# A conv–attention block in fp32 on one core: the order of the second pass, the last band's taps, and the place of its contraction

## The chip, the cores and the metric

The kernel runs on one core of one Trainium2 chip. The metric is the device time of one execution in microseconds, the median of several runs. Before the change: 3298.57 us, the median of three (3298.3 to 3300.13).

## The reference

The input is 8 images of 384 channels and 64 x 64 pixels, all in float32. Two layers follow each other, each added to its input:

```python
x = x + L0(_gn(x), Wq, bq, Wk, bk, Wv, bv, Wfc, bfc)     # linear attention
x = x + L1(_gn(x), fft_filter, w_in, w_dw, w_out)        # filter, depthwise conv, gate

# L0: conv1x1 = a 384 x 384 matrix over the channels, plus a bias; 6 heads of 64
q, k, v = rope(conv1x1(x, Wq, bq)), rope(conv1x1(x, Wk, bk)), conv1x1(x, Wv, bv)
q, k = elu(heads(q) * scale) + 1, elu(heads(k)) + 1
kv, k_sum = einsum('bhnd,bhne->bhde', k, v), k.sum(axis=2)
out = einsum('bhnd,bhde->bhne', q, kv) / (einsum('bhnd,bhd->bhn', q, k_sum) + 1e-6)
y0 = conv1x1(out, Wfc, bfc)
# L1
t = einsum('bchw,oc->bohw', x, w_in)
t = irfft2(rfft2(8 x 8 blocks of t) * fft_filter)
t = depthwise 3 x 3 convolution of t with w_dw, zero padding
y1 = einsum('bchw,oc->bohw', gelu(t[:, :192]) * t[:, 192:], w_out)
```

`_gn` is a group normalisation over 32 groups of 12 channels and all pixels. The keys and values of an image must be summed over all pixels before any output of L0 can be formed, and L0's result must be known over all pixels before L1's normalisation.

## The kernel before

An image is cut into 8 bands of 8 rows (512 pixels); a tile holds 384 channels as 3 blocks of 128 partitions by 512. Work on an image has a first pass (keys, values, their products; `k_project`, `v_project`, `kv_accumulate`), a second pass (`queries`, one call per image) and the L1 stage (the loop over `j` under `for b in range(nb)`). The first pass of image b+1 is woven into L1 of image b, so that TensorE has matmuls at all times. The last image's L1 has its own loop at the end.

The second pass handles a band in four steps. `q_project` (tile `pq`, 18 matmul records a band; every fp32 matmul shows as two) projects the queries, VectorE turns them (`turn`, L667, and L682, L684) and ScalarE and VectorE apply elu (`elu_plus_one`). `q_normalise` (tile `pn`) multiplies them with the key sums; VectorE and ScalarE form the reciprocal and split it into bfloat16 pieces (`rn`, `part`, `parts`, L701 to L709). `q_spread` (tile `prb`) spreads `parts` over the channels with bfloat16 matmuls and multiplies q by it on VectorE (L726). `project_out` (tile `pf`, 18 records a band) forms the product with the folded matrix `mt`; VectorE adds it to x (L738, `latest["sum"]`), and `band_sums` takes the statistics for L1's normalisation on ScalarE (L180, L183), the values of band 0 on VectorE.

Other work runs along in that pass. `late` is a generator, `last_band(b)`, with what remains of the previous image's last band of L1: its depthwise taps, gate and contraction; `next(late, None)` does one step of it. A tap is one of nine shifted products of the 3 x 3 filter: on VectorE one instruction per block of 128 channels (`tile_taps`, L839), or on ScalarE into a tile that a POOL transfer adds to the sum (`add_tap`, L823 and L825). `late_w` is a copy of the tap weights by way of a matmul with the identity (`pwd`). `chain` is `layer0_chain(b + 1)`: the next image's normalisation in small steps on VectorE (`far_chain`) with POOL transfers through DRAM in between, then the scaling of the key weights and the bias rows (`kvbias`).

After the second pass, `norm_chain(b, 1)` forms L1's normalisation in four steps (tiles `ps_m`, `ps_mc`, `ps_v`, `ps_r`, each with VectorE work behind it); between them `more` puts matmuls of the next image's keys (`pk`). Then `normalised` (tile `hf`) and the first matmuls of L1 (`pi`) follow. `contraction` (tile `pw`) is L1's last product; where the x tile is gone, its result is copied to `y` and a POOL transfer adds it to the output in DRAM.

The order on each engine is a planner's: it goes by the order of the text as priority and moves an instruction forward where by its own estimate the engine is free and the inputs are there. Within a block under `tc.issue_after(ins)`, instructions on the engine of `ins` come behind `ins`. `next(...)` on a generator does its work up to the next `yield`, so the `yield`s set the places in the text. PSUM has 8 tiles (`ps_tile`), the pool of work tiles `w` 9, that of `x` tiles 10, that of depthwise tiles `dw` 2.

## Time and profile before

The profiled execution took 3298.98 us; its span from the first to the last instruction is 3297.2 us.

| | busy us | share of the span |
|---|---|---|
| TensorE matmul (PE) | 3249.1 | 99% |
| TensorE weight load (PEld) | 1823.3 | 55% |
| VectorE (DVE) | 2724.7 | 83% |
| ScalarE (ACT) | 2040.4 | 62% |
| GpSimd (POOL) | 253.8 | 8% |

The granted clock of TensorE is 0.996 of full speed over the span. Matmuls are pipelined and their ends are modelled, so a record is longer than the distance to the next start; distances between starts are used below for what a group costs. A wait "A <- B" is the time that engine A stood idle until B's result came. "Issue" or a missing releaser means that the engine waited for nothing that the profile shows. SP issues the loads and stores, POOL the transfers that add and the small ones of the normalisation.

### The profile page before, as it was taken

Reading aid. Unit: us, or ns where it says so; the run is one execution under the profiler, and the core shown is the slowest. Engines: PE = TensorE matmul, PEld = TensorE weight load, DVE = VectorE, ACT = ScalarE, POOL = GpSimd, SP = SyncE. Lnnn points to the kernel's source line nnn. Section 1 sums busy time; section 2 is a strip of 40 time slices with the busy share of each in tenths; the row PEclk is TensorE's granted clock in tenths of the full one; section 3 lists DMA queues with packets and bytes.
Section 4 is the critical chain, followed back from the end, with each engine's and each line's share of the span. In section 5 each row is a group of like instructions: output and inputs, shape, how many; then the busy total and the mean of one; then the engine's idle time right before and its main releaser. Section 6 shows DMA issues by size and latency. Waiting matters only on the chain.

```text
span 3297.2 us, 53257 instructions
## 1 busy us (share of the span) xinstructions
PE 3249.1 (99%) x21133; PEld 1823.3 (55%) x21133; DVE 2724.7 (83%) x4480; ACT 2040.4 (62%) x4065; POOL 253.8 (8%) x381
## 2 busy tenths in 40 slices
PE   8999999999999999999999999999999999999998
PEld 5544666455664566645665456654566545665455
DVE  6577789978889789896888968899689987888767
ACT  4445666656766566655767556666566665556675
POOL 0000000000000000100001000010000100000064
PEclk9999999999999999999999999999999999999999
DMA  6324234452344524435235343354334542334113
GB/s 219 114 86 119 88 86 111 135 138 74 97 117 119 145 58 116 114 115 142 72 93 139 109 123 87 90 135 119 113 78 104 135 115 75 78 68 119 71 30 58
DMA packets 154445, 346.33 MB, mean 105 GB/s; under 512 B 29812, under 2 KB 41060, under 8 KB 146004
## 3 DMA queue, kind: packets, MB, share of 16 engines
q1 hardware_dynamic: 124500, 282.65, 26.3%
q0 software_dynamic: 29504, 60.06, 12.3%
q8 instruction: 166, 2.72, 0.3%
q14 instruction: 83, 0.68, 0.1%
q10 hardware_dynamic: 192, 0.21, 0.0%
HBM read 235.62 MB, written 99.93 MB: 102 GB/s over the span
## 4 chain that ended last, share of the span: by engine, by line
PE 92%; DVE 3%; ACT 3%; issue 1%; DMA 0%; SPq 0%; POOL 0%; DVEq 0%; ACTq 0%; POOLq 0%
PE pf L734 15%; PE pi L752 15%; PE pk L491 15%; PE pv L507 13%; PE pq L655 13%; PE pw L933 5%; PE pb L789 3%; PE pw L944 3%; PE acc L523 3%; PE pd L768 3%; PE acc L536 2%; PE pn L693 1%; ACT mt L570 1%; PE prb L717 1%; PE sums L865 1%
## 5 line engine op out<-in xcount | busy, mean ns | idle before, releaser
L839 DVE SCALAR_TENSOR_TENSOR dw<-ring,w_dw,dw 128x512 f32<-128x512 f32 x1225 | 858.7, 747 | 231.8 <-ACT ring L805 196.4
L491 PE MATMUL pk<-wk,x 128*128 128x384 f32 x1536 | 544.7, 496 | 0.0
L655 PE MATMUL pq<-x,wq 128*128 128x512 f32 x1152 | 521.6, 601 | 2.6 <-ACT mt L570 2.6
L752 PE MATMUL pi<-w_in,hf 128*128 128x384 f32 x1536 | 513.5, 491 | 5.5 <-ACT ring L799 4.2
L734 PE MATMUL pf<-qc,mt 128*128 128x512 f32 x1152 | 510.7, 597 | 0.0
L507 PE MATMUL pv<-wv,x 128*128 128x384 f32 x1344 | 470.0, 488 | 0.0
L752 PEld LDWEIGHTS pi<-w_in,hf 128*128 128x128 f32 x1536 | 288.0, 190 | 199.1 <-ACT ring L799 5.0
L491 PEld LDWEIGHTS pk<-wk,x 128*128 128x128 f32 x1536 | 283.5, 191 | 205.2 <-issue 32.2
L514 ACT COPY v<-pv 128x384 f32<-128x384 f32 x224 | 108.7, 485 | 424.5 <-PE pv L507 423.2
L734 PEld LDWEIGHTS pf<-qc,mt 128*128 128x128 f32 x1152 | 214.3, 190 | 255.5 <-issue 239.6
L507 PEld LDWEIGHTS pv<-wv,x 128*128 128x128 f32 x1344 | 253.6, 190 | 181.4 <-issue 8.4
L655 PEld LDWEIGHTS pq<-x,wq 128*128 128x128 f32 x1152 | 212.8, 190 | 250.6 <-issue 226.2
L738 DVE SCALAR_TENSOR_TENSOR x<-pf,bfc,x 128x512 f32<-128x512 f32 x192 | 138.6, 743 | 83.6 <-PE pf L734 83.2
L379 ACT ACTIVATE qs<-qc 128x512 f32<-128x512 f32 (+1 forms) x128 | 107.0, 836 | 144.1 <-DVE qc L684 143.7
L963 POOL DMA_DIRECT2D out_dram<-y x63 | 80.9, 1284 | 1446.6 <-DVE dw L839 799.0
L180 ACT ACTIVATE differences<-x,shift 128x512 f32<-128x512 f32 x168 | 120.0, 714 | 105.5 <-DVE x L738 105.5
L933 PE MATMUL pw<-gated,w_out 128*128 128x256 f32 x768 | 177.7, 380 | 3.2 <-DVE gated L849 2.0
L494 DVE TENSOR_TENSOR kc<-pk,kvbias 128x384 f32<-128x384 f32 x256 | 140.7, 550 | 40.6 <-PE pk L491 40.6
L933 PEld LDWEIGHTS pw<-gated,w_out 128*128 128x128 f32 x768 | 144.9, 190 | 43.7 <-issue 10.3
L759 ACT COPY ht<-pi 128x384 f32<-128x384 f32 x256 | 114.7, 483 | 68.2 <-PE pi L752 64.4
L379 ACT ACTIVATE ks<-kc 128x1536 f32<-128x1536 f32 x64 | 95.0, 1485 | 95.5 <-DVE kc L498 95.0
L374 ACT ACTIVATE hf<-x,nb,rs 128x512 f32<-128x512 f32 x192 | 146.1, 808 | 2.3 <-DVE nb L319 2.3
(216 smaller groups left out, 4555.4 us busy)
## 6 DMA issues: line engine op xcount, KB each, us to landing
tq<-in_tq SPq DMA_DIRECT2D x64, 1024.0 KB, 4.7
x<-in_x SPq DMA_DIRECT2D x64, 768.0 KB, 5.9
tk<-in_tk SPq DMA_DIRECT2D x64, 768.0 KB, 4.3
out_dram<-x SPq DMA_DIRECT2D x63, 768.0 KB, 3.5
out_dram<-y POOLq DMA_DIRECT2D x63, 768.0 KB, 7.7
xs<-in_x SPq DMA_DIRECT2D x56, 768.0 KB, 5.9
dw<-tap POOLq DMA_DIRECT2D x14, 512.0 KB, 6.4
wk<-in_wk SPq DMA_DIRECT2D x8, 576.0 KB, 3.8
```

The costliest lines, as they stand in the source:

```text
L180: nc.scalar.activation(out[:, m, :], x_[:, m, :], AF.Identity, bias=shift[:, m : m + 1], accum_out=of_m[0])
L374: nc.scalar.activation(dst, src, AF.Identity, bias=nb_[:, t : t + 1], scale=rs[:, t : t + 1])
L379: nc.scalar.activation(e, x_, AF.Relu, scale=-1.0)
L491: nc.tensor.matmul(pk[:, :C], tokens(t), wks[:, t, :], start=(t == 0), stop=(t == CT - 1))
L494: nc.vector.tensor_add(kc[:, i, :], pk[:, :C], bias)
L507: nc.tensor.matmul(pv[:, :C], xt[b, j][:, t, i * P : (i + 1) * P], wvs[:, t, :], start=(t == 0), stop=(t == CT - 1),)
L655: nc.tensor.matmul(p_, wqs[:, t, m * P : (m + 1) * P], xt[b, j][:, t, :], start=(t == 0), stop=(t == CT - 1),)
L734: nc.tensor.matmul(p_, mt[:, t, m * P : (m + 1) * P], q[:, t, :], start=(t == 0), stop=(t == CT - 1))
L738: latest["sum"] = nc.vector.scalar_tensor_tensor(xm, p_, bfc[:, m : m + 1], xm, ALU.add, ALU.add).ins
L752: nc.tensor.matmul(p_[:, :C], h[:, t, i * P : (i + 1) * P], w_in[:, t, :], start=(t == 0), stop=(t == CT - 1),)
L839: nc.vector.scalar_tensor_tensor(acc[:, m], src, wd, acc[:, m], ALU.mult, ALU.add)
L933: nc.tensor.matmul(p_[h][:, m - m0, :], w_out[:, 0, m * P : (m + 1) * P], gated[:, h * HT : (h + 1) * HT], start=(m == m0), stop=False,)
```

## The change

In `queries`, bands 2 to 7: the queries of band j+2 are projected without a cut, then band j-1's output product, then band j's spread, and band j+1's `q_normalise` directly behind it (for the last image from band 5 on, spread before output). The first spread comes behind the first third of band 3's queries. At band 7, two quarters of the next image's band 0 keys are projected ahead of the output product and the last spread; their VectorE work is put behind `parts`.

In `last_band`: taps 1 to 4 of all three blocks on ScalarE with a POOL transfer each, where it was taps 1 and 2 of two blocks; `late_w` and `pwd` go; VectorE's taps come behind the band's sum (block 0) or behind `parts` (blocks 1 and 2), the gate behind the last tap. The contraction of the last band moves to the norm chain of the following image, and its result is copied into the depthwise tile (`spare`) instead of an x tile.

In `far_chain` one `yield` moves, and the transfer of the shift is issued ahead of the read-back of the other; the scaling of the key weights and the bias columns come behind the last band's turned queries (`queried`); the scaling of the query weights behind the filter of band 4 in L1 (`filtered`). The first two loads of the next image's x are one band earlier.

```diff
@@ -333,7 +333,6 @@
         yield
-        yield
         mean, var = at[:, :, 0], at[:, :, 1]
@@ -355,10 +354,14 @@
         nc.gpsimd.dma_start(line.rearrange("(g k) -> g k", g=NG), var)
+        shift = scratch.tile([NG], F32, tag="shift", name=f"shift_line_{b}")
+        nc.gpsimd.dma_start(shift.rearrange("(g i) -> g i", i=1), minus)
         rs = small.tile([P, CT], F32, tag="rs0", name=f"rs0_{b}")
         nc.gpsimd.dma_start(rs, line.rearrange("(t p) -> p t", p=P))
-        params += rs, shift_to_all(b, minus)
-        for _ in range(4):
+        shift_bc = small.tile([P, NG], F32, tag="shift_bc", name=f"shift_bc_{b}")
+        nc.gpsimd.dma_start(shift_bc, shift.partition_broadcast(P))
+        params += rs, shift_bc
+        for _ in range(5):
             yield
@@ -664,7 +667,7 @@
         def turn(dst, src, m, table):
-            nc.vector.scalar_tensor_tensor(dst, src, m, table, ALU.add, ALU.mult)
+            return nc.vector.scalar_tensor_tensor(dst, src, m, table, ALU.add, ALU.mult).ins
@@ -677,7 +680,7 @@
             turn(qc[:, m, :], pq[m], bias[:, m : m + 1], tq[:, 2 * m, :])
-            turn(qs[:, 1 - m, :], pq[m], bias[:, m : m + 1], tq[:, 3 - 2 * m, :])
+            latest["queried"] = turn(qs[:, 1 - m, :], pq[m], bias[:, m : m + 1], tq[:, 3 - 2 * m, :])
             if m == 0:
@@ -706,7 +709,7 @@
         nc.scalar.copy(part, rn)
-        nc.vector.scalar_tensor_tensor(parts, part, take_off[:, 1:2], rn, ALU.mult, ALU.add)
+        latest["parts"] = nc.vector.scalar_tensor_tensor(parts, part, take_off[:, 1:2], rn, ALU.mult, ALU.add).ins
         return parts
@@ -773,7 +776,7 @@
             for i in range(2):
-                nc.vector.tensor_mul(tf[:, 2 * s + i, :], p_[i][:, :C], filt)
+                latest["filtered"] = nc.vector.tensor_mul(tf[:, 2 * s + i, :], p_[i][:, :C], filt).ins
         done.append(tf)
@@ -806,7 +809,7 @@
-    dw, diagonals = {}, {}
+    dw, spare, diagonals = {}, {}, {}
@@ -820,7 +823,8 @@
         for m in range(m0, CT):
-            nc.scalar.activation(t[:, m], ring[j % 2][:, m, 0:8, k : k + W], AF.Copy, scale=w_dw[:, m, k : k + 1])
+            src = ring[j % 2][:, m, k // 3 : k // 3 + 8, k % 3 : k % 3 + W]
+            nc.scalar.activation(t[:, m], src, AF.Copy, scale=w_dw[:, m, k : k + 1])
             first_on_vector[b, j, m] = k + 1
@@ -830,17 +834,17 @@
-    def tile_taps(b, j, m, weights, ks=None):
+    def tile_taps(b, j, m):
         t, acc = ring[j % 2], dw[b, j]
-        for k in ks or range(first_on_vector.pop((b, j, m), 1), 9):
+        for k in range(first_on_vector.pop((b, j, m), 1), 9):
             src = t[:, m, k // 3 : k // 3 + 8, k % 3 : k % 3 + W]
-            wd = weights[:, m, k : k + 1]
-            nc.vector.scalar_tensor_tensor(acc[:, m], src, wd, acc[:, m], ALU.mult, ALU.add)
+            wd = w_dw[:, m, k : k + 1]
+            latest["tapped"] = nc.vector.scalar_tensor_tensor(acc[:, m], src, wd, acc[:, m], ALU.mult, ALU.add).ins
...
         for m in range(CT):
-            tile_taps(b, j, m, w_dw)
+            tile_taps(b, j, m)
@@ -853,7 +857,7 @@
     def gate_taps(b, j):
-        af = dw.pop((b, j)).rearrange("p t r w -> p t (r w)")
+        af = spare[b, j] = dw.pop((b, j)).rearrange("p t r w -> p t (r w)")
         gate([af[:, m, :] for m in range(CT)])
@@ -949,7 +953,9 @@
             yield
-        y = xp.tile([P, CT, BT], F32, tag="x", name=f"y_{b}_{j}") if adding else None
+        y = spare.pop((b, j), None)
+        if j < NBAND - 1 and adding:
+            y = xp.tile([P, CT, BT], F32, tag="x", name=f"y_{b}_{j}")
         to = x_out[b][:, :, j * BT : (j + 1) * BT]
@@ -980,7 +986,7 @@
         yield from far_chain(b, params)
-        with tc.issue_after(latest["sum"]):
+        with tc.issue_after(latest["queried"]):
             scale_weight(wk, params)
@@ -992,6 +998,11 @@
             yield from c
+
+    def first_n(chain, n):
+        for _ in range(n):
+            next(chain)
+            yield
@@ -1056,7 +1067,10 @@
                     sum_weight(self.wq, "wq", scale)
-                scale_weight(self.wq, self.params, scale)
+                    scale_weight(self.wq, self.params, scale)
+                else:
+                    with tc.issue_after(latest["filtered"]):
+                        scale_weight(self.wq, self.params, scale)
                 if self.b == 0:
@@ -1092,36 +1106,51 @@
         mt = done[0]
-        q_spread(b, 0, q[0], normaliser.pop(0))
         project = q_project(b, 3, wq, qbias, q)
         next(project)
-        normalise(1)
+
+        def spread(j):
+            q_spread(b, j, q[j], normaliser.pop(j))
+            if j < NBAND - 1:
+                normalise(j + 1)
+
+        def output(j):
+            run(project_out(b, j, q.pop(j), mt))
+
+        spread(0)
         run(project)
-        run(project_out(b, 0, q.pop(0), mt))
-        q_spread(b, 1, q[1], normaliser.pop(1))
-        normalise(2)
+        output(0)
+        spread(1)
+        last = b == nb - 1
+        ahead = None
         for j in range(2, NBAND):
             if j < NBAND - 2:
-                project = q_project(b, j + 2, wq, qbias, q)
-                for _ in range(2):
-                    next(project)
-                normalise(j + 1)
-                run(project)
+                run(q_project(b, j + 2, wq, qbias, q))
                 next(chain, None)
-            q_spread(b, j, q[j], normaliser.pop(j))
-            output_ = project_out(b, j - 1, q.pop(j - 1), mt)
-            if j == NBAND - 2:
+            if last and j >= NBAND - 3:
+                spread(j)
+                output(j - 1)
+            elif j < NBAND - 1:
+                output(j - 1)
+                spread(j)
+            else:
+                after = Keys(b + 1, prepared)
+                ahead = after, after.project_k(0)
+                with tc.issue_after(latest["parts"]):
+                    for _ in range(2):
+                        next(ahead[1])
+                output_ = project_out(b, j - 1, q.pop(j - 1), mt)
                 next(output_)
-                normalise(j + 1)
-            run(output_)
+                spread(j)
+                run(output_)
             if j < NBAND - 2:
                 next(chain, None)
-            if j in (5, 7):
+            if j in (4, 6):
                 load_x(b + 1, j // 6)
...
         run(project_out(b, NBAND - 1, q.pop(NBAND - 1), mt))
-        return prepared
+        return ahead
@@ -1186,40 +1215,35 @@
-        for k in (1, 2):
-            add_tap(b, NBAND - 1, k, 1)
+        for k in range(1, 5):
+            add_tap(b, NBAND - 1, k, 0)
+            if k < 4:
+                yield
+        for m in range(CT):
+            with tc.issue_after(latest["parts" if m else "sum"]):
+                tile_taps(b, NBAND - 1, m)
+            if m == CT - 1:
+                with tc.issue_after(latest["tapped"]):
+                    gate_taps(b, NBAND - 1)
             yield
-
-        ps = ps_tile(f"pwd_{b}")
-        nc.tensor.matmul(
-            ps[:, : CT * 9], ident, w_dw.rearrange("p t k -> p (t k)"), start=True, stop=True
-        )
-        late_w = small.tile([P, CT, 9], F32, tag="late_w", name=f"late_w_{b}", bufs=1)
-        nc.vector.tensor_copy(late_w, ps[:, : CT * 9].rearrange("p (t k) -> p t k", t=CT))
-        yield
-        for m in range(CT):
             if m == 0:
-                tile_taps(b, NBAND - 1, m, w_dw, range(1, 8))
-                tile_taps(b, NBAND - 1, m, late_w, range(8, 9))
-            else:
-                tile_taps(b, NBAND - 1, m, late_w)
-            if m == CT - 1:
-                gate_taps(b, NBAND - 1)
-            yield
-        if b + 1 < nb - 1:
-            contract(b, NBAND - 1)
+                yield
+                yield
...
     for b in range(nb):
-        prepared = queries(b, keys, before_last, late)
-        keys = Keys(b + 1, prepared)
+        following = queries(b, keys, before_last, late)
         params = []
-        chain, more = norm_chain(b, 1, params), chain_of(keys.project_k(0), keys.load_values(), keys.project_k(1))
+        chain, more = norm_chain(b, 1, params), iter(())
         last = b == nb - 1
-        if last:
-
-            more = contraction(b - 1, NBAND - 1) if b else iter(())
-        for steps in (2, 0, 1, 1) if last else (2, 1, 1, 3):
+        if not last:
+            keys, first_keys = following
+            more = chain_of(first_keys, keys.load_values(), keys.project_k(1))
+        if b:
+            rest, more = more, contraction(b - 1, NBAND - 1)
+            if not last:
+                more = chain_of(first_n(rest, 4), more, rest)
+        for steps in (2, 0, 1, 1) if last else (2, 1, 1, 5) if b else (2, 1, 1, 2):
             next(chain)
...
                 next(more, None)
```

## The prediction

> **What bounds the kernel now.** I read the page's engine row first, then who waited for whom on TensorE, then TensorE's instructions in order of time through one image's second pass (image 3; images 1 to 6 repeat it every 402.35 us, pq of image 3 starting at 1369.41 and of image 4 at 1771.76), then busy time by stretch there. Columns: busy us (share of span) and count; total us, times, longest us; start, length, what, [idle before it, releaser]; a stretch, its length, and busy us of PE, PEld, DVE, ACT, POOL.

> ```profile
> PE 3249.1 (99%) x21133; PEld 1823.3 (55%) x21133; DVE 2724.7 (83%) x4480; ACT 2040.4 (62%) x4065; POOL 253.8 (8%) x381
> ...
> PE prb L717 <- DVE parts L709: 12.6, 14, 1.4
> PE ps_r L285 <- DVE rsg L314: 5.2, 9, 2.4
> ```

> ```profile
> 1394.05 7.89 PE L655 MATMUL pq<-x,wq 128*128 128x512 f32 x18
> 1403.33 0.35 PE L717 MATMUL prb<-parts,expand 32*128 32x128 bf16 x12 [1.39 <-DVE parts L709]
> 1403.60 2.84 PE L655 MATMUL pq<-x,wq 128*128 128x512 f32 x6
> 1406.38 0.86 PE L693 MATMUL pn<-qc,ks_bd 128*32 128x128 f32 x24
> 1407.17 5.42 PE L655 MATMUL pq<-x,wq 128*128 128x512 f32 x12
> 1412.42 7.89 PE L734 MATMUL pf<-qc,mt 128*128 128x512 f32 x18
> 1420.24 0.35 PE L717 MATMUL prb<-parts,expand 32*128 32x128 bf16 x12
> 1420.52 0.86 PE L693 MATMUL pn<-qc,ks_bd 128*32 128x128 f32 x24
> 1421.31 5.42 PE L655 MATMUL pq<-x,wq 128*128 128x512 f32 x12
> ...
> 1438.80 0.30 PE L1194 MATMUL pwd<-w_dw,groups 128*128 128x27 f32 x2
> ...
> 1447.84 0.35 PE L717 MATMUL prb<-parts,expand 32*128 32x128 bf16 x12
> 1448.11 7.99 PE L734 MATMUL pf<-qc,mt 128*128 128x512 f32 x18
> 1455.94 5.31 PE L655 MATMUL pq<-x,wq 128*128 128x512 f32 x12
> 1461.18 0.86 PE L693 MATMUL pn<-qc,ks_bd 128*32 128x128 f32 x24
> 1461.98 2.84 PE L655 MATMUL pq<-x,wq 128*128 128x512 f32 x6
> 1464.75 0.35 PE L717 MATMUL prb<-parts,expand 32*128 32x128 bf16 x12
> ```

> ```profile
> 1455.94:1472.86 16.92, 16.92 (x74) 7.44 (x72) 16.92 (x35) 12.02 (x25) 2.64 (x5) 1.00 0.39 94
> 1503.45:1522.97 19.52, 19.52 (x53) 9.04 (x49) 7.80 (x17) 11.49 (x28) 1.45 (x2) 1.00 0.65 155
> ```

> TensorE is the bound: 99% busy, and its repeats are near a fixed spacing (18 pf in 7.82 us between 1412.42 and 1420.24, 0.43 each). So time is won only where TensorE waits, where it turns from a full-array matmul to a small one and back, or where work leaves it. VectorE is full beside it in the bands (16.92 of 16.92 us) but has 11.7 us free in the last stretch; that distribution is what the change rearranges. I sum against the profiled run's 3298.98 us (span 3297.2), 0.41 above the median of 3298.57.

> **Start of the pass.** The first spread, prb(0), waits 1.39 us for parts(0); the chain of waits leads from there back through ScalarE's mt copies and two taps. The change puts the first third of pq(3) ahead of it (6 matmuls, 2.57 us) and pn(1) straight behind. Before, pq(2) to the rest of pq(3) is 1407.17 - 1394.05 = 13.12 us. After: 24 pq at 0.429 + 0.2 for two turns + prb 0.28 + pn 0.79 = 11.56. Gain 1.56 us. Cover: ScalarE's second tap grows from two tiles to three, 0.72 us (ScalarE tap row, 715 ns), so parts(0) may come 0.72 later than now; 1.39 + 0.72 = 2.11 is under 2.57. Taps 3 and 4 (2.1 us each) could be pulled forward to here; this order already ran VectorE's first taps of the last band 70 us ahead of their place in the text. Then prb(0) waits up to 2 us again. I take none, since ScalarE shows idle gaps of 4.1 and 2.6 us (1378.9 and 1403.8) to hold them.

> **The bands.** A band takes 16.91 us (1447.84 to 1464.75): pq cut by pn, prb, pf. The new band is pq, pf, prb, pn. Its pieces are all in the trace in that succession: pq 7.84 (1382.96 to 1390.80), pf behind pq 7.82, prb with pn behind it 0.28, pn with pq behind it 0.79 (1420.24 to 1421.31): 16.73. Gain 0.18 a band, 0.72 over bands 2 to 5. In addition prb(2) loses its wait of 0.40 (parts(2) now has 15.7 us of pq and pf in front of it; the chain rn to parts took 4.5 us at 1426.7), and pwd goes (0.14 to the next pq, 0.22 with its turn). The new order asks that q times prb(j-1) be ready when pf(j-1) starts 8.6 us later; on VectorE that is four instructions of 0.5 us, behind at most three sums of 0.75 us: 5 us late at worst by the rows of 1431 to 1438.5, so covered.

> **VectorE and ScalarE.** The last band's 20 taps on VectorE become 12: 8 x 0.747 = 6.0 us less, late_w's copy 0.18 less; wq's scaling, 1.1 us, goes from this stretch to the L1 stage behind "filtered". ScalarE gains 8 x 0.715 = 5.7 us and has 38% idle. None of it is on TensorE's path if the tail holds.

> **The tail.** pw of the last band (4.19 us at 1498.96) leaves for the norm chain; two quarters of the next image's keys (12 pk, 3.96) come in ahead of prb(7). Before, 1421.31 to ps_m at 1522.97 is 101.66 us. After: four bands 66.92; pf(5) 7.9, prb 0.28, pn 0.79; pk 3.96; pf(6) first third 2.67; prb 0.28; 30 pf 12.97; the other two quarters 3.96: 99.73. Gain 1.93, which contains the band gains, pwd and the prb(2) wait above. Cover of parts(7): pk + a third of pf = 6.6 us between pn(7) and prb(7), against 5.3 + 4.2 before. The nearest row is parts(7) now: pn done 1493.7, parts written 1501.4, 7.7 us, but with three taps, five q multiplications and wq's scaling between. These are gone or moved behind parts; I take 5 us, no wait; the far end is 7.7 - 6.6 = 1.1 us.

> Behind parts(7) now stand eight taps (m = 1 and 2), the gate, and the two key quarters' bias and turning. VectorE from parts(7) to ps_m: 8 x 0.747 = 6.0, gate 0.69 + 2 x 0.42 = 1.5, keys 2 x 0.55 + 2 x 0.95 = 3.0, q(7) 2.0, six sums 4.5, statistics 1.0: 18.0 us for about 18.5 (17.2 from prb(7) to ps_m, and the lead of parts). That is tight; bounds 0 to 6.0 us of lateness at ps_m (all taps ahead of the last sums). I take 0: back-to-back VectorE rows overlap by 0.07 to 0.1 us, so 18 is nearer 16.5.

> The keys' bias row must have landed for the first pk eviction. Its two POOL transfers took 10.5 and 4.4 us; the bias is now formed right behind the turns of pq(7), some 3 us earlier (about 1482 for 1485.1), so it lands near 1498 and the eviction is due near 1500. Its wait would be VectorE's own and reach TensorE only after 5 us (q(7) before pf(7)). I take 0.

> **The norm chain.** 1522.97 to pi at 1539.54 is 16.57 us. After: less 12 pk (3.9), plus pw 4.05, less the 0.20 wait at ps_r: 16.5. Gain 0.05. Between ps_v and ps_r lie now pw and a quarter of pk (6.2 us), with fewer VectorE instructions. But the finishing of the first keys (0.95 + 0.95 + 1.75 us on VectorE, 4.3 on ScalarE) now falls between ps_m and ps_v, where a single quarter of pk (2.1 us) covers each step. Bounds 0 to 3.5 us; I take 0.4.

> **DMA queues.** POOL issues four dw transfers of 768 KB an image for two of 512; they took 6.4 us at 512 KB (at most 9.9), say 10 each, in line on one tile, and VectorE's first tap comes only behind sum(2), 40 us after the second. On SP the second x tile no longer waits for y's transfer (71.9 us in all); y uses the depthwise tile, free again some 15 us after pw, before first_taps(b, 1). The far chain's shift and inverse transfers merely change order. All 0. [...]

> The gate's Gelu now runs in the tail between the band sums: two table loads there, 1.28 us each by the rows, into 8 us of idle ScalarE. [...]

> **Sum.** Images 1 to 6: 1.56 + 1.93 + 0.05 - 0.4 = 3.1 us each, 18.8. Image 7: 1.56, prb(2) 0.40, pwd 0.22, bands 0.72: 2.9. Image 0 has no late work: bands 0.72 and turns of the tail 0.5, but after ps_v only two quarters of pk for three, and none after ps_r: 1 to 3 us of wait. I take 0. Together 21.7: 3298.98 - 21.7 = 3277.3, against the median 3276.9; I say 3277. About 0.2% (6.6 us) is what a measurement of this kernel can tell from no change.

> **Rivals.** (1) The gain comes back in the norm chain: gm, mm and rsg each stand behind one VectorE instruction of 0.95 to 1.75 us. For it: ps_r waited already (5.2 us, 9 times). Against: the other two steps never waited over 1.2 us. Price 2 to 3.5 us an image, 12 to 21: 3289 to 3298. (2) Slower: the tail jams. Taps and gate run before the last sums, so the statistics and ps_m are late by up to 6 us. For it: 18.0 against 18.5 us, and ps_m today has only 0.4 us to spare (mv done 1522.60). It decides from 3.1 us an image on; at 6.0 it costs 7 x 6.0 - 21.7 = 20 over: 3319. (3) Nothing happens at the spreads: ScalarE's longer taps delay parts(0) by as much as the cover adds. Then 1.56 goes, 7 times: 3288.

> **Numbers.** The forecast with small deviations 0.60 (own range 3268 to 3287), rival 3 0.10, rival 1 0.13, rival 2 0.14, better than the forecast by more than 9 us (no new wait and image 0 too) 0.03. Range 3266 to 3302: rival 2's upper part is left out. Faster by over 0.2% (below 3292): 0.60 + 0.10 + 0.03 and under a third of rival 1, 0.77; within 0.2%: the rest of rival 1, 0.09; slower 0.14.

> **What the changed profile would show.** Right: prb waits for parts gone or under 4 us in all; bands 16.7 us apart; images 399 us apart; no pwd and late_w; L839's taps 1260 for 1316, tap transfers 28 of 768 KB; the tail's VectorE 16 us and more. Wrong if TensorE shows idle time at ps_m, ps_mc or ps_v, at prb(7) for parts, or at pf for q.

## The result, and the profile after

The kernel after the change takes 3325.89 us, the median of six runs (3324.36 to 3328.63), where six runs of the kernel before gave 3298.8: slower by 0.8%, ratio 1.0082 [1.0072, 1.0092]. The forecast was 3277 us. In the profiled execution the span is 3323.7 us; TensorE is busy for 98% of it, where it was 99%.

The distance from one image's first `pq` to the next one's, taken from the starts of the matmuls, is 402.35 us before and 406.15 to 406.24 after in images 1 to 6, where 399.2 was forecast; image 0 went from 405.6 to 409.38. So the loss is nearly the same in each of these images, 3.8 to 3.9 us, and 7 us an image separate forecast and result.

The chain of waits on TensorE after the change (engine, operation and line, what it waited for; us in all, times, longest):

```profile
PE ps_v L277 <- DVE d L302: 18.2, 9, 2.5
PE pf L737 <- DVE qc L729: 14.7, 14, 1.6
...
PE pn L696 <- DVE qc L670: 3.3, 7, 0.5
...
PE prb L720 <- DVE parts L712: 0.6, 1, 0.6
```

The 12.6 us at `prb` are 0.6 now, as was meant. In their place stand 36 us at `ps_v`, `pf` and `pn`. TensorE's timeline of image 3 shows where (start, length, operation, count; in brackets the idle time before it):

```profile
1405.67 10.46 PE L658 MATMUL pq<-x,wq 128*128 128x512 f32 x24
1416.07 0.35 PE L720 MATMUL prb<-parts,expand 32*128 32x128 bf16 x12
1416.89 0.86 PE L696 MATMUL pn<-qc,ks_bd 128*32 128x128 f32 x24 [0.47 <-DVE qc L670]
...
1498.37 0.35 PE L720 MATMUL prb<-parts,expand 32*128 32x128 bf16 x12
1498.64 0.86 PE L696 MATMUL pn<-qc,ks_bd 128*32 128x128 f32 x24
1501.13 7.99 PE L737 MATMUL pf<-qc,mt 128*128 128x512 f32 x18 [1.62 <-DVE qc L729]
...
1537.23 2.20 PE L494 MATMUL pk<-wk,x 128*128 128x384 f32 x6
1541.95 0.35 PE L277 MATMUL ps_v<-d,groups 128*32 128x1 f32 x6 [2.52 <-DVE d L302]
1542.23 4.54 PE L937 MATMUL pw<-gated,w_out 128*128 128x256 f32 x12
```

The first group is the start of the pass: prb(0) waits no longer, but pn(1) does, and pf(0) behind it another 0.47. The second is band 6: pf(5) comes 0.8 us behind prb(5), with only pn(6) between, and waits for the multiplications of q by that spread. Bands 2 to 5 have the 18 `pq` of the band after next in front of each `pf`; band 6 has none left to project. The third is the norm chain. VectorE's timeline at that place:

```profile
1538.43 0.14 DVE L298 TENSOR_SCALAR mm<-ps_mc 128x3 f32<-128x3 f32 x1
1538.54 1.76 DVE L501 TENSOR_TENSOR kc<-kc,ks 128x1536 f32<-128x1536 f32 x1
1540.21 0.16 DVE L300 TENSOR_TENSOR d<-mv,mm 128x3 f32<-128x3 f32 x1
1540.28 0.55 DVE L497 TENSOR_TENSOR kc<-pk,kvbias 128x384 f32<-128x384 f32 x1
1540.75 0.15 DVE L301 TENSOR_TENSOR d<-d 128x3 f32<-128x3 f32 x1
1540.87 0.96 DVE L477 TENSOR_TENSOR ks<-kc,tk 128x768 f32<-128x768 f32 x1
1541.75 0.15 DVE L302 TENSOR_TENSOR d<-d,mv 128x3 f32<-128x3 f32 x1
```

Three instructions of 0.15 us form `d`; three of the next image's first keys (1.76, 0.55 and 0.96 us) lie among them, while TensorE has one quarter of `pk`, 2 us, to do.

The last row of TensorE's fence is a fourth loss. Twelve `pw` take 4.48 us to the next start (1546.71). At the same place of image 1 they take 2.79:

```profile
731.25 0.35 PE L277 MATMUL ps_v<-d,groups 128*32 128x1 f32 x6 [2.46 <-DVE d L302]
731.53 2.86 PE L937 MATMUL pw<-gated,w_out 128*128 128x256 f32 x12
734.32 1.57 PE L948 MATMUL pw<-gated,w_out 64*128 64x256 f32 x12
```

The table by stretches of image 3, cut at 1542.37, has the cause (length; busy time of TensorE, weight load, VectorE, ScalarE and GpSimd, with counts; then the granted clock, the DMA engines' busy share and GB/s):

```profile
1538.96:1542.37 3.41, 0.89 (x9) 0.40 (x8) 3.41 (x7) 2.02 (x2) 0.00 (x0) 1.00 0.72 231
1542.37:1545.78 3.41, 3.41 (x9) 2.70 (x10) 1.65 (x3) 3.38 (x3) 0.00 (x0) 0.50 0.00 0
1545.78:1549.20 3.42, 3.42 (x20) 2.29 (x19) 1.26 (x6) 1.66 (x6) 0.00 (x0) 1.00 0.00 0
```

Behind the wait the granted clock is at half for one stretch of 3.41 us, which costs 1.69 us (4.48 against 2.79). Each of images 1 to 6 has one such stretch, behind `ps_v` in three and behind pf(5) in three; the kernel before had none between 0.21 and 3.13 ms.

For image 3, which stands for images 1 to 6, the parts nearly add up. The forecast had 0.4 of the 2.52 us at `ps_v` in it, so 2.12 are new there; 1.62 are at pf(5), 1.69 come from the clock, and 1.09 is what the start gained less than forecast (pq(2) to pf(0) took 18.37 us before and takes 17.90, a gain of 0.47 where 1.56 was forecast). That is 6.52 of some 7.0 us. The other half microsecond lies in no wait: the pieces of the new order take 0.10 us more behind pf(0), 0.15 in the tail and 0.27 in the norm chain than their sum in the forecast.

### The profile page after: what moved, and what is told of

The parts are those of the page before. It is cut to its first block, busy times and chain, and to the rows that moved or that the text cites. A ratio compares the mean times of both kernels' runs of the same rounds, so it can differ in the third digit from the quotient of the medians.

```text
span 3323.7 us, 53292 instructions
## 1 busy us (share of the span) xinstructions
PE 3252.5 (98%) x21119; PEld 1829.6 (55%) x21119; DVE 2698.6 (81%) x4417; ACT 2080.3 (63%) x4126; POOL 265.5 (8%) x395
## 4 chain that ended last, share of the span: by engine, by line
PE 89%; DVE 5%; ACT 4%; DMA 1%; issue 1%; SPq 0%; POOL 0%; DVEq 0%; ACTq 0%; POOLq 0%
PE pf L737 15%; PE pi L755 15%; PE pk L494 14%; PE pv L510 13%; PE pq L658 11%; PE pw L937 5%; PE pb L792 3%; PE pw L948 3%; PE acc L526 3%; PE pd L771 3%; PE acc L539 2%; PE pn L696 1%; ACT mt L573 1%; DMA wv<-in_wv 1%; DVE qc L729 1%
## 5 line engine op out<-in xcount | busy, mean ns | idle before, releaser
L843 DVE SCALAR_TENSOR_TENSOR dw<-ring,w_dw,dw 128x512 f32<-128x512 f32 x1260 | 884.4, 747 | 226.0 <-ACT ring L808 190.8
L658 PE MATMUL pq<-x,wq 128*128 128x512 f32 x1152 | 513.0, 599 | 2.8 <-ACT mt L573 2.8
L969 POOL DMA_DIRECT2D out_dram<-y x56 | 71.9, 1284 | 1270.9 <-DVE dw L843 798.5
L384 DVE SCALAR_TENSOR_TENSOR kc<-kc,ks 128x1536 f32<-128x1536 f32 x64 | 112.4, 1756 | 60.3 <-ACT ks L383 60.3
```

The lines of the kernel that those rows point to most:

```text
L658: nc.tensor.matmul(p_, wqs[:, t, m * P : (m + 1) * P], xt[b, j][:, t, :], start=(t == 0), stop=(t == CT - 1),)
L843: latest["tapped"] = nc.vector.scalar_tensor_tensor(acc[:, m], src, wd, acc[:, m], ALU.mult, ALU.add).ins
```

## The experiments

The theory: the two large waits are of the order's making, each a result that is due too soon behind the work that it depends on; the half clock follows from them. The rivals: VectorE is simply too full there, so that another order only moves a wait; or a load is late (the value weights `wv` landed 0.7 us after VectorE could have used them).

### The two waits

In all that follows the kernel before, run beside the others, had medians of 3298.8 to 3300.3 us. First the spread of bands 5 and 6 drawn ahead of the output product (as the last image has it):

```diff
-            if last and j >= NBAND - 3:
+            if j >= NBAND - 3 and (last or j < NBAND - 1):
                 spread(j)
                 output(j - 1)
```

> In bands 5 and 6 of every image the spread comes ahead of the output product, as the changed kernel has it for the last image alone. Theory (two waits make the loss: pf(5) stands directly behind prb(5) and pn(6) at band 6, where no query projection is left to cover the q products, 1.63 us in images 0 to 6; and ps_v waits 2.3 us for d): the pf(5) wait goes, 7 x 1.63 = 11.4 us, and with it up to three half-clock windows of 1.7 us, unless ps_v's wait draws them instead: 3310 to 3315 us, no idle time before pf(5), ps_v's wait unchanged. Rival (VectorE's tail is full, so that whatever wait is removed comes back at the next place): 3322 us or more, with the wait moved to prb(6), prb(7) or ps_m.

3359.52 us, ratio 1.0184 [1.0169, 1.0199]. The theory's range was missed; what came is the rival's sign, 3322 us or more with the wait moved to prb(6). TensorE's timeline of this version:

```profile
1517.54 1.45 PE L737 MATMUL pf<-qc,mt 128*128 128x512 f32 x3
1523.00 0.35 PE L720 MATMUL prb<-parts,expand 32*128 32x128 bf16 x12 [4.01 <-DVE parts L712]
1523.28 1.09 PE L696 MATMUL pn<-qc,ks_bd 128*32 128x128 f32 x24
```

pf(5) no longer waits, but prb(6) now comes only one output product behind pn(6), and waits 4.0 us for parts(6), with the granted clock at 0.50 behind it in images 1 to 6 (for 3.41 us in image 3, from 1523.77).

The same edit with another order of the chain, a single quarter ahead of the contraction:

```diff
-                more = chain_of(first_n(rest, 4), more, rest)
-        for steps in (2, 0, 1, 1) if last else (2, 1, 1, 5) if b else (2, 1, 1, 2):
+                more = chain_of(first_n(rest, 1), more, rest)
+        for steps in (2, 0, 1, 1) if last else (3, 1, 2, 4) if b else (2, 1, 1, 2):
```

> Both mended: spread first at bands 5 and 6, and in the norm chain of images 1 to 6 the order second key quarter's partner (third quarter), contraction, ps_m, contraction, ps_mc, rest of the contraction and the fourth quarter, ps_v, so that mm and d stand on VectorE ahead of all finishing of keys. Theory: both waits and the six half-clock windows go (11.4 + 14.4 + 10.2 us), some 1 us an image comes back at ps_mc, where three wv scalings stand ahead of gm: 3294 to 3300 us, at the kernel before. Rival (VectorE is full in the tail): 3312 us or more.

3349.7 us, ratio 1.0152 [1.0137, 1.0167], again in the rival's range. It carries the same wait at prb(6). In the norm chain `ps_v` does not wait any more in images 1 to 6, but the first `pi` does, for 2.4 us in each:

```profile
PE pi L755 <- ACT hf L377: 15.9, 7, 2.4
```

So this order of the chain only moves the wait. In the next version two quarters of `pk` precede the contraction in the chain, and all of the contraction comes before most of the remaining keys:

```diff
-                more = chain_of(first_n(rest, 4), more, rest)
-        for steps in (2, 0, 1, 1) if last else (2, 1, 1, 5) if b else (2, 1, 1, 2):
+                more = chain_of(first_n(rest, 2), more, rest)
+        for steps in (2, 0, 1, 1) if last else (2, 1, 2, 4) if b else (2, 1, 1, 2):
```

> The last band's contraction is spread between ps_m and ps_v, and the finishing of the first keys comes behind ps_v in the text. Theory (d stands behind the 1.76 us addition, the turning and the next evictions of the first keys on VectorE): most of ps_v's 2.3 us goes in images 1 to 6; one long addition is still between the parts of d, so about 1 us stays: 6 x 1.3 = 8 us less, and the half-clock windows at ps_v with it (0 to 5): 3313 to 3318 us; the pf(5) wait unchanged. Rival (what is late is the load of wv, which waits for mt's buffer and lands 0.7 us after VectorE asks for it): the same lateness shows at ps_mc or ps_v, 3324 us or more.

3304.49 us, ratio 1.0014 [1.0004, 1.0023]: 21.4 us of the 27 are back, more than expected. TensorE has 2.6 us of `pw` between ps_mc and ps_v instead of 2.2 of `pk`; mm comes 0.87 us behind the start of ps_mc instead of 1.96, since VectorE has fewer evictions in front of it, and two key instructions (0.95 and 1.76 us) lie among the steps of d instead of three. The wait at `ps_v` falls from 2.5 us to between 0.62 and 0.87 in images 1 to 6, 10.6 us in all; image 0, which the edit leaves as it was, still waits 2.44. With it go five of the six half-clock stretches (5 x 1.7 is 8.5 us). This edit alone can't tell more work on TensorE from less in VectorE's way.

The late load, tested by loading and scaling `wv` behind the variance:

```diff
-                scale_weight(self.wv, self.params)
+                with tc.issue_after(latest["var"]):
+                    scale_weight(self.wv, self.params)
...
-                more = chain_of(first_keys, keys.load_values(), keys.project_k(1))
+                more = chain_of(first_keys, keys.project_k(1))
...
-        run(chain)
+        run(chain, keys.load_values())
```

> Only the scaling of wv moves, behind var, so that no VectorE instruction ahead of gm or d waits for its load. Theory (the first keys' finishing is what delays d): at most the 0.7 us idle time and 1.1 us of scaling come off ps_v's wait, which stays over 1 us: 3318 to 3326 us. Rival (the load of wv is the cause): ps_v's wait goes altogether in images 0 to 6, 7 x 2.3 = 16 us and the half-clock windows there: 3305 us or less.

3327.24 us, ratio 1.0086 [1.0071, 1.0101], and `ps_v` waits 2.7 us in images 0 to 6. The load is not the cause.

Whether it is VectorE's order or the time between two steps that makes `ps_v` wait is told apart by leaving TensorE's order alone and putting only the end of the first keys (L501 and the ELU behind it) after the variance:

```diff
+        def finish():
+            nc.vector.tensor_add(kc, kc, ks)
+            elu_plus_one(kc, ks)
+
+        if b and j == 0:
+            held.append(finish)
...
+                with tc.issue_after(latest["var"]):
+                    held.pop()()
```

> The changed kernel (3325.9 us) with TensorE's order untouched; only the addition and the ELU that finish the next image's first keys (1.76 us and more on VectorE) are put behind the variance of the norm chain, where they stood between mm and d. Theory (ps_v waits 2.5 us because VectorE, in order, is busy with the keys when mm comes): the wait falls under 0.7 us, seven times about 2 us, and with it the half-clock stretches behind it, three of 1.75 us: 3306 to 3313 us. Rival (the steps from ps_mc to d take that long by themselves, and only more work on TensorE between them helps, as the contraction did in the first comparison): 3320 us or more.

3313.71 us, ratio 1.004 [1.0027, 1.0054]: 12 us less, just above the theory's range, with no wait at `ps_v` in images 0 to 6. VectorE forms `d` in one go, and TensorE, with its order unchanged, starts `ps_v` without a wait (the first three rows are VectorE's):

```profile
1539.95 0.14 DVE L298 TENSOR_SCALAR mm<-ps_mc 128x3 f32<-128x3 f32 x1
1540.12 0.16 DVE L300 TENSOR_TENSOR d<-mv,mm 128x3 f32<-128x3 f32 x1
1540.52 0.16 DVE L302 TENSOR_TENSOR d<-d,mv 128x3 f32<-128x3 f32 x1
1541.03 0.35 PE L277 MATMUL ps_v<-d,groups 128*32 128x1 f32 x6
```

So the keys' instructions between the steps of `d` are the cause, and other work for TensorE at that place is one cure, another order on VectorE a second. Images 1 to 6 gained 2.5 to 3.5 us each, image 0 lost 5.9: it has no contraction, and there ps_r and the first `pi` waited 2.9 and 2.7 us.

### pf(5), and the row that was nearly late

From here on the base is the version with the contraction first, 3304.5 us. Band 5's spread goes ahead of pf(4), and pn(6) stays behind it, so that 18 `pf` stand between prb(5) and pf(5), and another 18 between pn(6) and prb(6):

```diff
+            elif j == NBAND - 3:
+                q_spread(b, j, q[j], normaliser.pop(j))
+                output(j - 1)
+                normalise(j + 1)
             elif j < NBAND - 1:
```

> The order of the norm chain that gave 3304.5 us (the last band's contraction first), with prb(5) drawn ahead of pf(4) and pn(6) left behind it, so that eighteen pf stand between prb(5) and pf(5). Theory (pf(5) waits because only pn(6), 0.8 us, stands between the spread and the output of the same band, while its four multiplications need 2 us): the wait of 1.63 us, seven times 11.4 us, and the half-clock stretch behind one of them (1.8 us) go: 3290 to 3295 us. Rival (VectorE is behind there, by the scaling of wk and the bias terms that the change put ahead of the sums of band 4, and the order on TensorE only moves the wait to prb(6), as it did where prb(6) went ahead of pf(5) too: 4.0 us an image there): 3302 us or more, with prb(6) waiting for parts.

3300.87 us, ratio 1.0002 [0.9993, 1.0011]. The wait at pf(5) is gone, and prb(6) does not wait; but only 3.6 us came of some 13, for pf(7) waits now, 0.86 us in image 3: neither the theory's range nor the rival's. The other cure tried at pf(5) was to take wk's scaling, which the change had put ahead of band 4's sums, off VectorE there:

```diff
         with tc.issue_after(latest["queried"]):
-            scale_weight(wk, params)
             cols = bias_columns(b, params[1], 0, 3 * CT)
...
         yield
+        with tc.issue_after(latest["spread"]):
+            scale_weight(wk, params)
```

Here `latest["spread"]` is the last multiplication of a band's q by its spread.

> The same base of 3304.5 us, TensorE's order unchanged; only wk's scaling (three instructions, 1.07 us of VectorE) is put behind the four multiplications of band 5. Theory (distance): the multiplications can't start before prb(5) is done, so they come at most about 0.5 us earlier, and pf(5) still waits 1.1 us or more: 3300 to 3303 us. Rival (the backlog of VectorE): the wait shrinks by the whole 1.07 us, seven times 7.5: 3297 us or less.

3305.06 us, ratio 1.0017 [1.0008, 1.0026]: no gain, and pf(5) still waits 1.63. In image 3 the multiplications start 0.77 us behind prb(5)'s start with wk's scaling ahead of them and without it, and take 1.94. Distance decides there, not the load on VectorE.

What made pf(7) wait was first put down to the keys' eviction and turning, and the second key quarter was moved behind prb(7), its VectorE work behind band 7's multiplications:

```diff
                 with tc.issue_after(latest["parts"]):
-                    for _ in range(2):
-                        next(ahead[1])
+                    next(ahead[1])
                 output_ = project_out(b, j - 1, q.pop(j - 1), mt)
                 next(output_)
                 spread(j)
+                with tc.issue_after(latest["spread"]):
+                    next(ahead[1])
                 run(output_)
```

> On the version with the contraction first and prb(5) ahead of pf(4) (3300.9 us): the second of the two key quarters is moved behind prb(7), its eviction and turning behind band 7's multiplications. Theory (what that version left, 0.86 us at pf(7), seven times, comes from the first keys' eviction and turning, 3 us of VectorE between sum and multiplication): the wait goes, 3293 to 3296 us. Rival (the turning is only moved on to the last sums and ps_m, or prb(7), with 4.7 us of TensorE's work ahead of it instead of 6.6, waits for parts): 3300 us or more.

3315.07 us, ratio 1.0039 [1.0026, 1.0052], worse by 14 us. The waits that answer to it:

```profile
PE ps_m L277 <- DVE mv L205: 9.5, 6, 1.6
...
PE pf L737 <- DVE qc L729: 5.5, 11, 0.8
```

pf(7) still waits, and the keys' work, now behind band 7's multiplications, makes the statistics and `ps_m` late, as the rival had it. Two versions built on this one keep that wait. The first adds the late finish shown above:

> The version with the keys apart, and the finish of the first keys behind the variance as well. Theory (the remaining wait of 0.62 us at ps_v is the 1.76 us addition between two steps of d): 3 to 5 us less than the version with the keys apart alone, 3288 to 3293 us. Rival (the finish then stands in the way of ps_r or of the first values): the same time or more.

3310.22 us, ratio 1.0031 [1.002, 1.0041]: 5 us less, of the size expected, from a base 20 us above the one assumed. The second adds another place for the second tap:

```diff
-        next(late, None)
         normalise(0)
...
         output(0)
+        with tc.issue_after(latest["sum"]):
+            next(late, None)
         spread(1)
```

> The version with the finish late too, and the second tap of the last band (three tiles, 1.95 us of ScalarE) taken from its place between mt's copies to behind the first output. Theory (ScalarE is what pn(1) and pf(0) wait for by way of VectorE, 0.47 us each, since that tap stands in front of mt's copies and band 2's bias): 4 to 7 us less, 3282 to 3288 us. Rival (VectorE is full there, whatever ScalarE does): the same time within 2 us.

3306.11 us, ratio 1.0018 [1.0009, 1.0027], with runs from 3297 to 3315. The waits at pn(1) and pf(0) are gone in it, the one at ps_m is not.

The cause of what is left is in VectorE's timeline of the version with only the finish moved, which has the same wait at pf(7) (line numbers 7 higher than in the kernel after):

```profile
1514.27 0.74 DVE L850 SCALAR_TENSOR_TENSOR dw<-ring,w_dw,dw 128x512 f32<-128x512 f32 x1
1516.62 0.56 DVE L498 TENSOR_TENSOR kc<-pk,kvbias 128x384 f32<-128x384 f32 x1 [1.61 <-DMA kvbias<-bias_line]
...
1521.28 0.74 DVE L748 SCALAR_TENSOR_TENSOR x<-pf,bfc,x 128x512 f32<-128x512 f32 x1
1521.94 1.94 DVE L736 TENSOR_TENSOR qc<-qc,prb 128x384 f32<-128x384 f32 x4
```

VectorE stands 1.61 us for the next image's bias row, ahead of everything that band 7 needs, and pf(7) waits 1.52 us in this image. The row's path is long, in the kernel after (queue instructions of image 3):

```profile
L436 POOL DMA_DIRECT2D bias_line<-bias x1: 860/860/860, 1498.0 to 1498.0; - x1
L437 POOL DMA_DIRECT2D kvbias<-bias_line x1: 571/571/571, 1509.3 to 1509.3; - x1
```

3 KB to DRAM take 11.0 us, the row back 4.4, so it is there at 1513.7; its first reader starts at 1514.97, when VectorE is free for it. In the kernel after, the row is on time by 1.3 us. In the version above it landed later (6.2 us for the read), and in the others its reader came up earlier; VectorE stood 6.3 us (18 `pf` between), 7.7 (finish moved) and 18.3 us (keys apart) in all. The cure is to form the row a band earlier (wk's scaling, which comes in the same step, moves with it):

```diff
-        for _ in range(5):
+        for _ in range(3):
             yield
```

On the version with 18 `pf` between prb(5) and pf(5):

> The version with the contraction first and prb(5) ahead of pf(4) (3300.9 us), with the next image's bias row and wk's scaling formed behind the turns of pq(6) instead of pq(7), one band (16.7 us) earlier. Theory (what was left at pf(7), 0.86 us in most images, 4.8 us in all, comes from VectorE standing 6.3 us in all for the bias row's transfers, in line ahead of band 7's multiplications): both go, 3294 to 3297 us. Rival (the keys' eviction and turning, 3 us of VectorE, are what stands in the way, whenever the row lands): 3300 us or more.

3294.82 us, ratio 0.9983 [0.9974, 0.9992]: 6.0 us less than without it; VectorE no longer stands for the row, and pf(7) waits no more. On the one with only the finish moved:

> The version with the keys' finish behind the variance (3313.7 us), whose VectorE stood 7.7 us in all for the bias row, with the same row a band earlier. Theory: the new waits at pf(7) go, 5.8 us in all: 3306 to 3309 us. Rival (the landing is not the cause): 3312 us or more.

3307.3 us, ratio 1.0023 [1.0014, 1.0031]: 6.4 us less. And on the kernel after itself:

> The changed kernel (3325.9 us) with the bias row and wk's scaling a band earlier and nothing else. Theory (its waits at pf(5) and ps_v come from the order, and its row landed in time): at most the 0.5 us by which that work delays band 5's multiplications, seven times: 3322 to 3327 us. Rival (those 2.1 us of VectorE, put ahead of band 4's sums by the change, are the cause at pf(5)): 3315 us or less.

3326.25 us, ratio 1.0082 [1.0066, 1.0097]: alone it does nothing. The row was no cause of the loss, but it would have taken back 6 us of what the other cures gain.

### The start of the pass

Two changes to the start, each on the base of 3304.5 us. First the order of the kernel before:

```diff
         project = q_project(b, 3, wq, qbias, q)
-        next(project)
...
-            if j < NBAND - 1:
+            if 0 < j < NBAND - 1:
                 normalise(j + 1)
...
         spread(0)
+        next(project)
+        normalise(1)
         run(project)
```

> The same base of 3304.5 us with the start of the pass as in the kernel before: prb(0) ahead of the first third of pq(3), pn(1) behind that third. What the prediction took for this part, 1.56 us an image, would make it 12.5 us slower: 3317 us. What the two traces show, some 0.5 us an image: 3308 to 3309 us. Rival (the new start is worth nothing, since its two waits of 0.47 us at pn(1) and pf(0) took the place of the one at prb(0)): 3304 us or less.

3306.96 us, ratio 1.0022 [1.0014, 1.0031]: prb(0) waits its 1.39 again, pn(1) and pf(0) do not. The new start is worth 0.3 us an image by this, 0.5 by the traces (pq(2) to pf(0)).

Then pn(1) behind all of pq(3), with prb(0) left where the change put it:

```diff
-            if j < NBAND - 1:
+            if 0 < j < NBAND - 1:
                 normalise(j + 1)
...
         spread(0)
         run(project)
+        normalise(1)
```

> The same base of 3304.5 us; prb(0) stays behind the first third of pq(3), but pn(1) goes behind its last third, ahead of pf(0). Theory (pn(1) waits 0.47 us for a PSUM tile and its chain of five small VectorE instructions stands ahead of the rest of band 0's multiplications): both waits go, up to 0.93 us an image: 3297 to 3301 us. Rival (VectorE is full there, whatever the order: pq(3)'s own thirds then wait for the same tile, or prb(1) for parts(1)): 3304 us or more.

3342.99 us, ratio 1.0133 [1.0119, 1.0146]: the rival came true on both counts. The wait of 0.47 us is now at the rest of pq(3), pf(0) keeps its own, and prb(1) waits for parts(1), in spite of the output product in between:

```profile
1438.52 0.38 PE L720 MATMUL prb<-parts,expand 32*128 32x128 bf16 x12 [3.45 <-DVE parts L712]
```

VectorE had the rest of band 0's multiplications and pq(3)'s turns in front of rn(1): 8.0 us from pn(1)'s start (1425.72) to its first instruction there (1433.71).

### All cures together

Contraction first, prb(5) ahead of pf(4), the row a band earlier, the finish behind the variance, the second tap behind the first output (key quarters together, as in the change):

> All cures together on the changed kernel: contraction first, prb(5) ahead of pf(4), bias row a band earlier, the keys' finish behind the variance, the second tap behind the first output. Theory (each took or takes its own wait: pf(5), pf(7), ps_v 0.62 us, pn(1) and pf(0) 0.47 us each): 3283 to 3291 us, faster than the kernel before. Rival (VectorE has no room left in the tail, and the wait comes out at ps_m, 1.6 us an image, as in the version with the keys apart): 3297 us or more.

3286.82 us, ratio 0.996 [0.9948, 0.9973], faster than both kernels: in images 1 to 6 each cure took its wait. One more edit leaves image 0's finish where it was:

```diff
-        if b and j == 0:
+        if b > 1 and j == 0:
             held.append(finish)
```

> The version with all cures (3286.8 us), with the keys' finish put behind the variance from the second image's chain on and left as it was in image 0's, which has no contraction to lie under it. Theory (image 0 took 414.1 us for 409.8 us in the versions without the late finish, by waits at ps_r and pi and the half clock behind them): some 4 us less, 3281 to 3284 us. Rival (image 0's delay is made up of something else): 3286 us or more.

3280.83 us, ratio 0.994 [0.9927, 0.9954]: 6.0 us less by the medians, 3.8 between the two profiled runs, of which image 0 has 2.8. Its largest waits on TensorE:

```profile
PE px L457 <- DMA x<-in_x: 7.2, 3, 6.1
PE ps_r L285 <- DVE rsg L315: 4.4, 3, 2.3
PE pi L762 <- ACT ring L809: 4.2, 6, 1.3
PE ps_v L277 <- DVE d L302: 3.7, 3, 2.5
```

No `pf`, `pn` or `prb` is among them; of these only one `prb` of the last image waits, 0.6 us. VectorE is busy for 2699.5 us in all, where it was 2698.6 in the kernel after, so the rival that VectorE is simply too full is out: with the same work in another order TensorE has no wait above 0.15 us in images 1 to 6. These take 399.22 to 399.32 us each, 3.1 less than before, which is the gain per image that the prediction worked out; image 0 takes 411.32, 5.7 more than before (2.5 us of wait at `ps_v`, 0.7 at `ps_r`, and behind the first of them twelve `pk` that take 7.20 us where the kernel after has 4.14). In image 0 the expectation was met only in part (411.3 where 409.8 was expected).

## Why the prediction was wrong

**The start of the pass** failed in size. Its step "24 pq at 0.429 + 0.2 for two turns + prb 0.28 + pn 0.79" counts TensorE's work and asks only whether parts(0) is ready. pn(1) needs a PSUM tile that VectorE frees (0.47 us), and pf(0) the products of band 0 (0.47 us), both behind the same stretch of ScalarE: the second tap, 1.95 us, stood between mt's copies. The tap's growth was counted, but against prb(0) alone, and pn(1) and pf(0) were taken as ready. In the versions with the tap moved both waits are gone, and pq(2) to pf(0) gains 1.65 us: TensorE's work was summed rightly, the readiness was not. Rival 3 (nothing at the spreads) came near in size, but not in its reason: parts(0) was in time.

**The bands** were right where pq is projected: 1432.56 to 1449.28 is 16.72 us for 16.73 forecast, prb(2)'s wait and pwd are gone. The step that failed is "the new order asks that q times prb(j-1) be ready when pf(j-1) starts 8.6 us later ... so covered". It was worked out for bands with a `pq` and applied to all; at band 6 the 8.6 us are 0.8. The tail's own sum, in which "pf(5) 7.9" follows the last band directly, had the two operations side by side. This is 11.4 us of wait in images 0 to 6, and three of the half-clock stretches.

**VectorE and ScalarE** and **the DMA queues** held: 1260 taps for 1316, 28 transfers of 768 KB at 7.0 us, no wait for a tap. The Gelu table load is 1.28 us in the trace after too.

**The tail** held at the places that it named: parts(7) came without a wait, `ps_m` too. So rival 2 did not happen in the kernel after. It did in the version with the keys apart (1.6 us at `ps_m`), so 0 lateness was right with little to spare: in image 3 of the kernel after the last instruction of mv ends at 1534.00, and `ps_m` starts at 1534.06. For the bias row, "I take 0" was right as well, and so was "its wait would be VectorE's own", but the step "reach TensorE only after 5 us" was not tested by the kernel after: in the shorter versions 1.61 us of it became 1.52 us at pf(7).

**The norm chain** failed most. The step "a single quarter of pk (2.1 us) covers each step" took each step as one key instruction long, with 3.5 us as the far end and 0.4 taken. Between mm and the last d lay three of them, 3.27 us together; from mm's start to the end of the last d 3.47 us went by. The measured wait was 2.3 to 2.5 us an image: rival 1's mechanism, at its own price of 2 to 3.5 us, though at `d`, which it did not name, and beside two losses that it did not have. Image 0, "1 to 3 us of wait. I take 0", became 3.8 us longer, with 2.28 at `ps_v` and 0.70 at `ps_r`. Image 7, from its first `pq` to the end, went from 318.4 to 317.8 us where a gain of 2.9 was forecast: 1.1 of the missing 2.3 us is the start, about 0.5 the bands, with a wait of 0.6 at prb(6), and the rest lies behind `ps_m` and was not traced to a cause. Six images at 7.0 us, image 0 at 3.8 and image 7 at 2.3 make 48 of the 49 us between forecast and result.

**What no step had** is the clock: six stretches at half clock, 1.7 us each, 10.2 us. The sum charged a wait with its own length only. Idle time at `ps_v` and at `pf` for q stood in the prediction as signs of being wrong, and both came; what they would cost did not.

The rivals were priced one at a time; what came was the mechanism of rival 1 at its price, most of rival 3, and two costs that no rival had, the wait at pf(5) and the clock. The size of the gain, 3.1 us an image, is what images 1 to 6 show once these are cured, in a kernel with five further moves that the prediction did not have. That it agrees to 0.1 us is partly luck: the start gives 1.65 us for 1.56, pf(0) to `ps_m` 1.63 for 1.93, the norm chain loses 0.15 for 0.35.

## What to carry to other kernels

For each operation that is moved, find in the new order what it depends on, and measure the work between the two in every trip of the loop, the last ones above all, where the filler has run out. When a wait in front of the bound engine is taken away, ask which chain of transfers was hidden behind it: here a bias row that was on time by 1.3 us. Where an engine takes its instructions in order, as VectorE did here (it stood 1.61 us for the bias row, and band 7's sum and multiplications came behind it), a long instruction of another task can hold up a chain of short steps: three of 1.76, 0.55 and 0.96 us lay between steps of 0.15 us, and TensorE waited 2.5 us. And a wait on TensorE can cost more than its length: of the six waits of 1.62 to 1.63 us at pf(5) in the kernel after, three cost another 1.7 us in clock.

## What the runs showed of the hardware

Waits of one length were not all followed by it. In the kernel after, all six waits at pf(5) were 1.62 to 1.63 us long and began 1.51 to 1.57 us behind the border of a cell, and three were followed; what decided between these six stays open. The waits of 3.45 us at prb(1), with pn(1) behind all of pq(3), and of 4.0 us at prb(6), with the spread drawn ahead, were always followed by it between 0.3 and 3.1 ms (13 of 13); the 1.39 us at prb(0) in the kernel before never were.
